# Reciprocal roots of normalisation statistics as powers on GpSimd, in a four-layer convolution block

## The chip, the cores and the metric

The kernel runs on one core of a Trainium2 chip. The metric is device time in microseconds (us) of one execution, as the median of several runs; less is better. Engines are named TensorE (PE; PEld is its loading of weights), VectorE (DVE), ScalarE (ACT), GpSimd (POOL) and SyncE (SP, which only issues DMAs here).

## The reference

The input x is 16 images of 64 channels and 128 x 128 pixels, float32. Four layers follow each other. Each normalises its input by groups (32 groups of two channels, per image) and adds its result to what came in:

```python
def _gn(v, G=32, eps=1e-5):
    g = v.reshape(B_, G, C_ // G, H_, W_)
    m = jnp.mean(g, axis=(2, 3, 4), keepdims=True)
    s = jnp.var(g, axis=(2, 3, 4), keepdims=True)
    return ((g - m) / jnp.sqrt(s + eps)).reshape(v.shape)

x = x + _L0_conv_ref(_gn(x), L0_conv_conv_w)      # gram matrix of the channels, two 64 x 64 products
x = x + _L1_conv_ref(_gn(x))                      # two 3 x 3 edge filters, sum of absolute values
x = x + _L2_conv_ref(_gn(x), L2_conv_W, L2_conv_b)  # shift by one pixel of half the channels, 3 x 3 conv
x = x + _L3_conv_ref(_gn(x), ...)                 # 3 x 3 conv, 1 x 1 conv, batch norm over all images, clip
```

The division by `jnp.sqrt(s + eps)` in `_gn` is what the change touches. The batch norm at the end has a root of its own, which it does not touch.

## The kernel before

Layers 0 and 1 are one stage, `Front`: the matrix of layer 0 and both normalisations are folded into one 128 x 128 product (`abd`) and one pair of scale and offset per channel, and the edge filters are then done by VectorE and ScalarE. `Layer2` and `Layer3` are stages with 3 x 3 convolutions on TensorE. A stage `Gram` makes the gram matrix of an image from x alone, and from it the coefficients of layers 0 and 1.

The work goes in steps, and a step in four quarters (`q` from 0 to 3). An image takes eight steps of a stage. In one step, image b is in `Front`, an earlier one in `Layer2` and a still earlier one in `Layer3`, 10 steps behind each other, with the gram matrix of a coming image beside them. The order of instructions on every engine is the one in which they are written (`InOrder` keeps it); each engine takes its own in that order and waits by semaphores for what they need.

The statistics are handled by chains, Python generators that do one link per `tick()` at the end of a quarter:

- `gram_chain` (line 313), once per image, has two roots: the first (line 347) without an epsilon, for layer 0, and the second (line 425), for layer 1, into the tile `co1`.
- `coefficients` (line 288) runs twice per image: at the end of `Front`, for layer 2, with the argument `back` (the bias), into `co2`; and at the end of `Layer2`, for layer 3, into `co`.

So there are four roots per image and 64 in all, each made by `rstd` (line 270). `mE` holds mean and mean square of each channel, in PSUM. `rstd` copies them to `me`, takes `nv` = mean squared minus mean square (the negative variance), subtracts the epsilon, has ScalarE take the root `sd`, and then, a quarter later (after the `yield`), has VectorE take the reciprocal `r0` and refine it: r = r0 * (1.5 + 0.5 * nv * r0 * r0). The offset `co[:, 1:2]` follows, and where the root itself is wanted (layers 1 and 2 keep the un-normalised input in the sum) another reciprocal makes it from r. For layer 2 it is also masked by channel (`left`, `right`).

GpSimd has this work in the steady state: in quarter 1 of each step of `Layer2`, four operations `edges` (lines 873 to 878) and two on border columns of `v` (lines 881 and 882), and, twice per step, a pair of DMAs from its queue that copy `d` into its shifted twin `qd` (`twin`, line 810). `Layer3` makes the same kind of twin with ScalarE copies (line 952). TensorE reads `d`, `qd` and `v`. VectorE makes each `d` by `difference` (line 706), and reads `edges` when it takes a result of layer 2 out of PSUM.

After the last image the statistics of the batch norm are complete, and a tail reads two arrays back from DRAM, normalises, adds and writes the output.

Of the kernel before, what the change touches and what calls it, by code (L numbers as in the profile page):

```python
# [11 lines left out]
AF = mybir.ActivationFunctionType  # L12
ALU = mybir.AluOpType
# [3 lines left out]
P = 128  # L17
# [7 lines left out]
GN_EPS = 1e-5  # L25
# [19 lines left out]
def single(table, n):  # L45

    for o in range(2):
        planes = [i for m, i, half, _ in table if (m, half) == (n, o)]
        if len(planes) == 1:
# [2 lines left out]


NAMES = [("I", P), ("same", P), ("all", P), ("gavg", P), ("gmean", P), ("bnavg", P), ("Id", C), ("q", 1),
         ("keep0", 1), ("keep1", 1), ("left", 1), ("right", 1), ("I3", 3 * P), ("lower", 1), ("upper", 1)]
AT = {}
K_END = 0
for _n, _w in NAMES:
# [19 lines left out]
def constants():  # L78
    k = np.zeros((P, K_END), np.float32)
    p = np.arange(P)  # L80
    ch = p % C

    def put(name, a):
        k[:, AT[name][0]:AT[name][1]] = a

    same = ch[:, None] == ch[None, :]
    pair = ch[:, None] // 2 == ch[None, :] // 2
    put("I", np.eye(P))
    put("same", same)
    put("all", np.full((P, P), 0.5))  # L90
    put("gavg", 0.25 * pair)
    put("gmean", pair / (2.0 * HW))
    put("bnavg", (ch[:, None] == (p // 2)[None, :]) / (B * HW))
    put("Id", ch[:, None] == np.arange(C)[None, :])
    put("q", 0.25)
    put("keep0", (~((ch >= C // 4) & (ch < C // 2)))[:, None])
    put("keep1", (~(ch < C // 4))[:, None])

    left, right = ch < C // 4, (ch >= C // 4) & (ch < C // 2)
    put("left", left[:, None])  # L100
    put("right", right[:, None])
    put("I3", np.concatenate([np.eye(P) * m[:, None] for m in (left, ~left & ~right, right)], axis=1))
    put("lower", (p < C)[:, None])
    put("upper", (p >= C)[:, None])
    return k
# [3 lines left out]
def tile_kernel(ctx: ExitStack, tc: tile.TileContext, x, cw_h, w2_t, b2, wbin_t, w1_t, b1, gamma, beta, consts, out):  # L109
    nc = tc.nc  # L110
    pe, dve, act, sp, pool = (InOrder(tc, e) for e in (nc.tensor, nc.vector, nc.scalar, nc.sync, nc.gpsimd))
# [8 lines left out]
    def k(name):  # L120
        return kc[:, AT[name][0]:AT[name][1]]
# [41 lines left out]
    def sv(name, n=1):  # L163
        return small.tile([P, n], F32, tag=name, name=name)
# [6 lines left out]
    def small_product(dst, wt, src):  # L171

        for o in (1 - last[0], last[0]):
            pe.matmul(dst[cols(o)], wt[:, cols(o)], src, start=True, stop=True)
        last[0] = o
# [5 lines left out]
    def sm(n, rows=P):  # L181
        if n > 8:
            return bank[0:rows, P:P + n]
        turn[0] = (turn[0] + 1) % 16
        return bank[0:rows, 8 * turn[0]:8 * turn[0] + n]
# [73 lines left out]
    def when(who):  # L259

        while turn_of[0] % 2 != who:
            yield
# [4 lines left out]
            if next(c, chains) is chains:  # L267
                chains.remove(c)

    def rstd(mE, r, me, eps=None):  # L270

        dve.tensor_copy(me, mE)
        nv = sv("nv")
        dve.scalar_tensor_tensor(nv, me[:, 0:1], me[:, 0:1], me[:, 1:2], op0=ALU.mult, op1=ALU.subtract)
        if eps is not None:
            dve.tensor_scalar_sub(nv, nv, eps)
        sd = sv("sd")
        act.activation(sd, nv, AF.Sqrt, scale=-1.0)
        yield
        r0 = sv("r0")  # L280
        dve.reciprocal(r0, sd)

        e = sv("e")
        dve.scalar_tensor_tensor(e, nv, r0, r0, op0=ALU.mult, op1=ALU.mult)
        dve.tensor_scalar(e, e, 0.5, 1.5, op0=ALU.mult, op1=ALU.add)
        dve.tensor_mul(r, r0, e)

    def coefficients(st, put, back=None):

        s2 = sv("s2", 2)  # L290
        dve.tensor_reduce(s2, st, axis=AX.X, op=ALU.add)
        yield
        yield from when(TENSOR)
        pm = sm(2)
        small_product(pm, k("gmean"), s2)
        yield
        co = sv("co", 2) if back is None else sv("co2", 6)
        me = sv("me", 2)
        r, mean = co[:, 0:1], me[:, 0:1]
        yield from rstd(pm, r, me, GN_EPS)  # L300
        dve.scalar_tensor_tensor(co[:, 1:2], mean, -1.0, r, op0=ALU.mult, op1=ALU.mult)
        if back is not None:

            dve.reciprocal(co[:, 2:3], r)
            dve.tensor_mul(co[:, 3:4], co[:, 2:3], k("left"))
            dve.tensor_mul(co[:, 4:5], co[:, 2:3], k("right"))
            dve.tensor_add(co[:, 5:6], mean, back)
        put(co)


# [2 lines left out]
    def gram_chain(b, pg):  # L313
# [29 lines left out]
        pm = sm(2)  # L343
        small_product(pm, k("gavg"), st)
        yield
        r, me = sv("r"), sv("me", 2)
        yield from rstd(pm, r, me)

        vv = sv("vv", 3)
# [69 lines left out]
        pm = sm(2)  # L419
# [2 lines left out]

        co = stp.tile([P, 5], F32, tag="co1", name=f"co1_{b}", bufs=EARLY + 3)
        r, mean = co[:, 0:1], co[:, 3:4]
        yield from rstd(pm, r, co[:, 3:5], GN_EPS)
        dve.scalar_tensor_tensor(co[:, 1:2], bias, mean, r, op0=ALU.subtract, op1=ALU.mult)
        dve.reciprocal(co[:, 2:3], r)
        lead[b] = abd, co

    def gram_product(pg, w, first, end):  # L430
# [16 lines left out]
    def first_gram():  # L447
# [30 lines left out]
        for link, _ in enumerate(gram_chain(0, pg)):  # L478
            if link in (2, 3, 4, 5, 6):
                rows_to_columns(1, link - 2, rows[link - 2])  # L480

    class Gram:
# [5 lines left out]
        def at(self, i, q):  # L488
            b = self.b
            n = 4 * (i - NS) + q  # L490

            self.part({1: 44, 5: 42, 9: 42}.get(n, 0))
            if n == 10:
                chains.append(gram_chain(b, self.pg))

            if i == 2 and q == 0:
                for m in range(3):
                    self.load(m)
            m = {11: 0, 13: 1, 15: 2, 19: 3, 21: 4, 23: 5, 27: 6, 31: 7}.get(4 * i + q)
            if m is not None:  # L500
                rows_to_columns(b, m, self.xr.pop(m))
                if m + 3 < NS:
                    self.load(m + 3)
# [45 lines left out]
    class Front:  # L549
# [56 lines left out]
        def at(self, i, q):  # L606
            b = self.b
            if q == 0:
                if i == -3:

                    self.xe = xin.tile([P, W], F32, tag="xe", name=f"xe_{b}", bufs=1)
                    sp.dma_start(self.xe[lo], x[b][:, HH, :])
                    sp.dma_start(self.xe[hi], x[b][:, HH - 1, :])
                    sp.dma_start(x2_d[b][0:W].rearrange("(p w) -> p w", p=1), w0[0:1, 0:W])
                if i + 3 < NS and i + 3 not in self.xs:
                    self.load(i + 3)
                if -1 <= i < NS - 1:
                    self.prepare(i + 1, 1)
                if 1 <= i:
                    self.store(i - 1)  # L620
                    act.activation(
                        junk.rearrange("p (j w) -> p j w", w=W), self.x2.pop(i - 1), AF.Square,
                        accum_out=self.st[:, 1, i - 1:i],
                    )
                if i == NS:
                    chains.append(coefficients(self.st, lambda co: coefs2.update({b: co}), b2_sb))
# [140 lines left out]
    class Layer2:  # L767
# [65 lines left out]
        def at(self, i, q):  # L833
# [3 lines left out]
            if q == 0:  # L837
                if i == NS:
                    chains.append(coefficients(self.st, self.done))
                if 1 <= i:  # L840
                    two = self.p.pop(i - 1)[0]

                    e = self.edges.pop(i - 1).rearrange("p t (m n) -> p n m t", n=2)
                    ends = two[:, :, :, 0:W:W - 1]
                    dve.tensor_add(ends, ends, e)
                    x3 = ring.tile([P, 2, CP, W], F32, tag="x3", name=f"x3_{b}_{i - 1}", bufs=NS + 2)
                    tiles3[b].append(x3)
                    dve.scalar_tensor_tensor(
                        x3.rearrange("p s j w -> p s (j w)"), two.rearrange("p s j w -> p s (j w)"), 1.0,
                        self.c.unsqueeze(1).to_broadcast([P, 2, CP * W]),  # L850
                        op0=ALU.mult, op1=ALU.add, accum_out=self.st[:, 0, i - 1:i],
                    )
                if 0 <= i < NS:
                    difference("d2", 0, self.v[i], m)
                    self.twin(0)
# [267 lines left out]
    pm = sm(2)  # L1123
    pe.matmul(pm, k("bnavg"), mv, start=True, stop=True)
    me = cpool.tile([P, 2], F32, name="me_bn")
# [4 lines left out]
    sd = cpool.tile([P, 1], F32, name="sd_bn")  # L1130
    act.activation(sd, var, AF.Sqrt)
    r0 = cpool.tile([P, 1], F32, name="r0_bn")
    dve.reciprocal(r0, sd)
    e = cpool.tile([P, 1], F32, name="e_bn")
# [56 lines left out]
```

## Time and profile before

| | us |
|---|---|
| three runs | 2726.27, 2729.09, 2729.88 |
| median | 2729.09 |
| profiled execution, span from first to last instruction | 2727.2 |
| PE busy | 2162.2 (79%) |
| DVE busy | 2170.0 (80%) |
| ACT busy | 2079.2 (76%) |
| POOL busy | 852.7 (31%) |

The profile gives the profiled execution by its span; no other time of that execution is given, and the span is 1.9 us under the median of the runs. The span divides into stages: up to 45 us the first image's gram matrix and coefficients, then the stages filling up one behind another, then all of them running together, and after about 2280 us the tail.

The shares of busy time are means over these stages, so a stage has to be looked at by itself. In a row of a timeline the figures are the start and the duration in us, then engine, line, operation and tiles (`out<-in`), and in brackets how long the engine had been idle and what ended that. Line 73 is the helper `InOrder`, through which nearly all instructions pass, so they are told apart by tile. A row of a list of waits gives the total in us, the number of waits and the longest. A group's row in an answer by tile gives minimum, median and maximum duration in ns.

### The profile page before, as it was taken

The page shows a single profiled execution, that of the slowest core. Times are in us where ns is not written, and L with a number is a line of the kernel's source. Part 1 is how long each engine was busy: PE and PEld are TensorE (multiplying, and loading weights), DVE is VectorE, ACT ScalarE, POOL GpSimd, SP SyncE. Part 2 cuts the span into 40 slices and gives each one's busy share as a digit, 9 for nine tenths or more (in the row PEclk, how much of TensorE's full clock was granted, in tenths as well). Part 3 has the DMA queues.
Part 4 walks back from the last instruction along what each step waited for, and adds up shares of the span by engine and source line. Part 5 has one row for each costly group of instructions (what it writes and reads, how often), then busy time and mean ns, then how long its engine had stood idle before and what let it go on. Part 6 is the DMA issues. An engine that isn't in the chain of part 4 may idle for free. (4 is left out here: it accounts for less than half of the span.)

```text
span 2727.2 us, 45742 instructions
## 1 busy us (share of the span) xinstructions
PE 2162.2 (79%) x14804; PEld 913.7 (34%) x14804; DVE 2170.0 (80%) x3495; ACT 2079.2 (76%) x3065; POOL 852.7 (31%) x1350
## 2 busy tenths in 40 slices
PE   6578899999999999999999999999999993000000
PEld 4234433434343434343434343333334641000000
DVE  4999999899999999999999999999995335333332
ACT  4766889898989898989898989899997667333332
POOL 2045424443434243333343334445453200000000
PEclk8689999999999999999999999999999996555555
DMA  8799878888888888888888887888877868999999
GB/s 199 205 239 239 226 197 239 225 235 225 235 228 237 227 226 229 226 227 234 225 224 237 214 204 203 207 211 216 224 200 186 226 188 314 420 420 420 420 420 385
DMA packets 693598, 685.93 MB, mean 252 GB/s; under 512 B 60096, under 2 KB 580448, under 8 KB 693360
## 3 DMA queue, kind: packets, MB, share of 16 engines
q1 hardware_dynamic: 668208, 613.83, 76.4%
q0 software_dynamic: 25152, 69.18, 10.0%
q8 instruction: 119, 1.95, 0.3%
q14 instruction: 119, 0.97, 0.1%
HBM read 346.23 MB, written 268.44 MB: 225 GB/s over the span
## 5 line engine op out<-in xcount | busy, mean ns | idle before, releaser
L73 PE MATMUL two<-d,w 128*64 128x508 f32 (+2 forms) x2560 | 848.9, 587 | 0.0
L73 PE MATMUL two<-d,wi 128*64 128x508 f32 (+3 forms) x1536 | 573.8, 577 | 0.0
L73 PE MATMUL two<-qd,pk 128*64 128x512 f32 (+1 forms) x1024 | 520.0, 589 | 24.5 <-DMA qd<-d 16.6
L73 POOL DMA_DIRECT2D qd<-d x512 | 271.1, 532 | 852.8 <-DVE d L73 323.9
L73 POOL TENSOR_SCALAR edges<-v,co 64x8 f32<-64x8 f32 x512 | 340.2, 664 | 349.0 <-ACT v L73 216.8
L73 DVE TENSOR_TENSOR d<-v 128x512 f32<-128x512 f32 (+1 forms) x512 | 346.6, 680 | 65.3 <-issue 37.5
L73 PEld LDWEIGHTS two<-d,w 128*64 128x64 f32 x2560 | 278.7, 136 | 320.0 <-issue 270.9
L73 PE MATMUL one<-v,w 128*64 128x508 f32 (+2 forms) x1600 | 364.3, 579 | 1.1 <-ACT v L73 1.1
L73 PE MATMUL one<-v,wi 128*64 128x508 f32 (+3 forms) x1536 | 353.3, 591 | 2.0 <-issue 1.4
L73 ACT COPY qd<-d 64x512 f32<-64x512 f32 x512 | 315.4, 616 | 19.9 <-DVE d L73 13.8
L73 DVE SCALAR_TENSOR_TENSOR e<-e 128x1032 f32<-128x1032 f32 (+1 forms) x256 | 313.0, 1223 | 0.0
L73 ACT ACTIVATE xh<-po,co 128x128 f32<-128x128 f32 (+1 forms) x480 | 275.9, 624 | 23.9 <-PE po L73 21.4
L73 PEld LDWEIGHTS two<-d,wi 128*64 128x64 f32 x1536 | 178.0, 135 | 197.4 <-issue 180.0
L73 DVE SCALAR_TENSOR_TENSOR y<-two,c 128x1024 f32<-128x1024 f32 x128 | 156.0, 1219 | 97.8 <-ACT v L73 45.6
L73 POOL TENSOR_SCALAR v<-v,kc 128x9 f32<-128x9 f32 x256 | 213.4, 847 | 12.0
L73 PE MATMUL po<-x,abd 64*64 64x512 f32 (+1 forms) x1024 | 177.1, 640 | 45.6 <-ACT xh L73 42.2
L73 ACT ACTIVATE v<-x,co 128x1024 f32<-128x1024 f32 (+3 forms) x256 | 203.8, 847 | 0.0
L73 ACT ACTIVATE u<-u 128x1024 f32<-128x1024 f32 x128 | 135.5, 1059 | 75.6 <-DVE u L73 74.6
L73 PEld LDWEIGHTS two<-qd,pk 128*64 128x64 f32 x1024 | 131.6, 135 | 176.9 <-issue 85.5
L73 PEld LDWEIGHTS one<-v,w 128*64 128x64 f32 x1600 | 130.9, 136 | 175.3 <-issue 146.5
L73 ACT ACTIVATE c<-one,co 128x512 f32<-128x512 f32 x128 | 86.7, 678 | 127.4 <-PE one L73 124.0
L73 DVE SCALAR_TENSOR_TENSOR u<-xh 128x1170 f32<-128x1170 f32 x128 | 175.4, 1370 | 4.2 <-ACT xh L73 4.1
(165 smaller groups left out, 3325.2 us busy)
## 6 DMA issues: line engine op xcount, KB each, us to landing
x<-in_x SPq DMA_DIRECT2D x256, 256.0 KB, 4.6
x_d<-u SPq DMA_DIRECT2D x512, 128.0 KB, 4.0
y_d<-y SPq DMA_DIRECT2D x512, 128.0 KB, 3.8
x_d<-x SPq DMA_DIRECT2D x496, 128.0 KB, 2.7
xr<-in_x SPq DMA_DIRECT2D x120, 512.0 KB, 5.9
qd<-d POOLq DMA_DIRECT2D x256, 130.0 KB, 3.3
qd<-d POOLq DMA_DIRECT2D x256, 129.8 KB, 3.8
v<-x_d SPq DMA_DIRECT2D x448, 72.1 KB, 3.0
```

Of the source, the lines that this page charges most:

```text
L73: return self.tc.keep_in_program_order(call(*args, **kwargs))
```

## The change

`rstd` no longer uses ScalarE, and VectorE's part ends with `nv`. GpSimd takes `va` = eps - `nv` and then r = `va` to the power -0.5, with the exponent from a new constant of two columns, `half`; where the root is wanted, it takes `va` to the power 0.5. For layer 2 the masked roots and the sum of mean and bias are moved from VectorE to GpSimd too. VectorE's offset `co[:, 1:2]` stays after the `yield`, and reads r.

```diff
@@ NAMES
-         ("keep0", 1), ("keep1", 1), ("left", 1), ("right", 1), ("I3", 3 * P), ("lower", 1), ("upper", 1)]
+         ("keep0", 1), ("keep1", 1), ("left", 1), ("right", 1), ("I3", 3 * P), ("lower", 1), ("upper", 1), ("half", 2)]
@@ constants
+    put("half", np.array([-0.5, 0.5]))
@@ rstd
-    def rstd(mE, r, me, eps=None):
+    def rstd(mE, r, me, eps=0.0, root=None):
 
         dve.tensor_copy(me, mE)
-        nv = sv("nv")
+        nv, va = sv("nv"), sv("va")
         dve.scalar_tensor_tensor(nv, me[:, 0:1], me[:, 0:1], me[:, 1:2], op0=ALU.mult, op1=ALU.subtract)
-        if eps is not None:
-            dve.tensor_scalar_sub(nv, nv, eps)
-        sd = sv("sd")
-        act.activation(sd, nv, AF.Sqrt, scale=-1.0)
+        pool.tensor_scalar(va, nv, -1.0, eps, op0=ALU.mult, op1=ALU.add)
+        pool.tensor_tensor(r, va, k("half")[:, 0:1], op=ALU.pow)
+        if root is not None:
+            pool.tensor_tensor(root, va, k("half")[:, 1:2], op=ALU.pow)
         yield
-        r0 = sv("r0")
-        dve.reciprocal(r0, sd)
-
-        e = sv("e")
-        dve.scalar_tensor_tensor(e, nv, r0, r0, op0=ALU.mult, op1=ALU.mult)
-        dve.tensor_scalar(e, e, 0.5, 1.5, op0=ALU.mult, op1=ALU.add)
-        dve.tensor_mul(r, r0, e)
@@ coefficients
-        yield from rstd(pm, r, me, GN_EPS)
+        yield from rstd(pm, r, me, GN_EPS, None if back is None else co[:, 2:3])
         dve.scalar_tensor_tensor(co[:, 1:2], mean, -1.0, r, op0=ALU.mult, op1=ALU.mult)
         if back is not None:
 
-            dve.reciprocal(co[:, 2:3], r)
-            dve.tensor_mul(co[:, 3:4], co[:, 2:3], k("left"))
-            dve.tensor_mul(co[:, 4:5], co[:, 2:3], k("right"))
-            dve.tensor_add(co[:, 5:6], mean, back)
+            pool.tensor_add(co[:, 5:6], mean, back)
+            pool.tensor_mul(co[:, 3:4], co[:, 2:3], k("left"))
+            pool.tensor_mul(co[:, 4:5], co[:, 2:3], k("right"))
         put(co)
@@ gram_chain
-        yield from rstd(pm, r, co[:, 3:5], GN_EPS)
+        yield from rstd(pm, r, co[:, 3:5], GN_EPS, co[:, 2:3])
         dve.scalar_tensor_tensor(co[:, 1:2], bias, mean, r, op0=ALU.subtract, op1=ALU.mult)
-        dve.reciprocal(co[:, 2:3], r)
         lead[b] = abd, co
```

## The prediction

> **What bounds the kernel now.** I read the table of windows first, since one figure for the whole span mixes stages with different limits. Columns: length, then busy us of PE, PEld, DVE, ACT, POOL, the granted clock, DMA share, GB/s.
>
> ```profile
> 30.00:45.00 15.00, 8.59 (x90) 4.96 (x88) 6.85 (x39) 7.96 (x11) 0.00 (x0) 0.66 0.95 273
> ...
> 100.00:150.00 50.00, 29.45 (x444) 19.10 (x444) 49.16 (x76) 35.05 (x50) 2.04 (x3) 0.70 0.78 197
> 150.00:300.00 150.00, 122.11 (x1174) 58.62 (x1170) 141.05 (x269) 104.65 (x146) 82.48 (x100) 0.92 0.93 238
> ...
> 1000.00:1500.00 500.00, 494.72 (x3546) 203.43 (x3543) 472.77 (x802) 450.59 (x691) 183.80 (x310) 1.00 0.86 228
> ...
> 2320.00:2727.00 407.00, 0.00 (x0) 0.00 (x0) 126.23 (x103) 127.64 (x103) 0.00 (x0) 0.50 1.01 414
> ```
>
> Four stages: to 45 us a serial chain (no engine is busy), to 300 us VectorE (49.16 of 50, 141.05 of 150), to about 2210 us TensorE (494.72 of 500), and at the end DMA alone. The changed roots stand in the first three; the tail, also written with ScalarE's root, is left as it is.
>
> Then the timeline around one root of layer 3 in TensorE's stage:
>
> ```profile
> 958.37 0.15 DVE L73 TENSOR_SCALAR nv<-nv 128x1 f32<-128x1 f32 x1
> 958.44 0.68 DVE L73 TENSOR_TENSOR d<-v 128x512 f32<-128x512 f32 x1
> ...
> 958.55 0.20 ACT L73 ACTIVATE sd<-nv 128x1 f32<-128x1 f32 x1 [0.83 <-DVE nv L73]
> ...
> 959.04 1.28 DVE L73 SCALAR_TENSOR_TENSOR u<-e,co,u 128x1024 f32<-128x1024 f32 x1
> ...
> 960.85 0.16 DVE L73 RECIPROCAL r<-sd 128x1 f32<-128x1 f32 x1
> ...
> 961.68 0.16 DVE L73 SCALAR_TENSOR_TENSOR co<-me,co 128x1 f32<-128x1 f32 x1
> ...
> 962.14 1.24 ACT L73 COPY qd<-d 64x512 f32<-64x512 f32 x2
> ...
> 963.44 0.64 PE L73 MATMUL two<-qd,pk 128*64 128x512 f32 x1 [0.70 <-ACT qd L73]
> ```
>
> See three things. ScalarE stood 0.83 us until nv came. VectorE came back for the root 2.33 us later (958.52 to 960.85) without a wait, and spent 0.83 us on four dependent small operations. TensorE lost 0.70 us because ScalarE's copy qd was late. The last is one of TensorE's few waits, by the list of waits of 430 to 1760 us:
>
> ```profile
> PE two L73 <- ACT qd L73: 7.0, 13, 0.7
> PE two L73 <- DMA qd<-d: 6.6, 10, 1.3
> ```
>
> The price of a small GpSimd operation is that of edges (minimum, median, maximum):
>
> ```profile
> L73 POOL TENSOR_SCALAR edges<-v,co x512: 302/320/3487, 152.2 to 2176.2; 64x8 f32<-64x8 f32 x171
> ```
>
> **What the Trainium skill says.** "SBUF — State Buffer", section "Who interferes with whom": a VectorE instruction with two SBUF inputs and a GpSimd instruction that reads SBUF exclude each other, and the second to issue blocks. The trace agrees: the median of edges is 0.32 us but the groups give a mean of 0.664, and the first four, beside VectorE's u and e of 1.2 us each, took 7.47 us together. "GPSIMD Engine Reference", section 2.1: the first call into freshly loaded code pays about 6 us. In the built program one library instruction stands ahead of GpSimd's first TENSOR_SCALAR in both kernels. Before, that was at 152.21 us, 0.1 us after its input, so the load hid in 43.9 us of idleness; now it follows the memset at 21.67 us, with 12 us until the first nv at 33.79. I count nothing. "ScalarE: Activation LUTs", "What ACT_TABLE_LOAD costs": 1283 ns per load; the trace has one of 1283 ns, and it stays, since the start and the tail still take a Sqrt. No page prices a power on GpSimd, and the trace has none.
>
> **The unknown.** Call p the time of one undisturbed 128x1 power. Below, 0.30 us (the fastest edges; no power is quicker than a multiply). Above, 4.8 us: the GPSIMD page's section 2 gives a core 16 partitions, and if its code took them one after another at a whole small operation each, 16 x 0.30. I take 0.8: one vector of 16 lanes, and two to three simple operations' worth of steps.
>
> **The change by parts.** VectorE loses 384 instructions: 64 each of reciprocal (156 ns), e (220), e (154) and product (159), which by starts is 0.83 us per root; 48 subtractions of 154; 32 reciprocals into co; 32 products and 16 additions of some 155. By kind, per root: 0.8 us (first root of a Gram chain, no epsilon), 1.15 (its second), 1.5 (layer 2), 1.0 (layer 3); 16 of each. ScalarE loses 64 roots of 0.20 us and the waits for nv, 36.5 us in 30 places. GpSimd gains 208 instructions, no DMA: 64 va, 64 powers, 32 root powers, 48 for left, right and the bias. SP's queue is passed by nothing.
>
> The new wait: VectorE's product into co waits for the first power alone (the second is awaited by no near VectorE instruction). The latency is hand-over, va, hand-over, power, hand-over: 0.07 + 0.32 + 0.07 + p + 0.07 = 0.53 + p undisturbed, 0.07 being the step from edges to edges. Beside VectorE's long operations, va and the power each end at an operation's end. Behind va on GpSimd stand edges, the border columns of v and the twin DMAs; VectorE's d waits for those columns.
>
> *First chain (to 45 us), serial.* First root: VectorE goes on at once with vv, which doesn't need r; 33.79 to 34.77 us drops out, -1.0; r is wanted at 36.88 and is there at 35.1. Second: nv at 41.79 to co at 43.08 was 1.29 us, becomes 0.53 + 0.8 = 1.33. Sum **-0.9**.
>
> *45 to 300 us, VectorE.* Eleven roots (4, 4, 2, 1 of the kinds): 4 x 0.8 + 4 x 1.15 + 2 x 1.5 + 1.0 = 11.8 us of VectorE less. New stalls, by the time from nv to the use in the trace: the four first roots have none (r is used a product later); of the others, those with 5.67 and 7.12 us have none; 4.62 and 2.85 us about 0.5 each; 2.51 and 1.72 us 0.2 + p = 1.0 each (va takes the time of VectorE's own operations, then the power is bare); 1.12 us (148.43) 0.5 + p = 1.3. Together 4.3, net -7.5. VectorE is 94% the bound there: **-6.8** (bounds -9 at p = 0.3, +11 at 4.8).
>
> *300 to 2210 us, TensorE.* VectorE's and ScalarE's saved time is covered by TensorE's work. What counts is TensorE's 7.0 us of waits for qd, nearly all behind a root of layer 3, where ScalarE now runs 0.9 us earlier: -6.5. Against that, a root of layer 3 stalls VectorE for 0.2 + p = 1.0, just what it saves. After a chain's second root, the power and the root power stand before edges, which start up to 1 us later; the columns were ready 3.7 us before VectorE's d, so that is hidden. At other steps d waits already (15 times, 4.0 us), but no root is there. For twin DMAs, which TensorE waits for at times (6.6 us), I add 1.5. Sum **-5.0**. End (layer 3 at 2205.8 us): 1.53 becomes 1.5; ScalarE earlier by 0.3: **-0.3**.
>
> Total -0.9 - 6.8 - 5.0 - 0.3 = **-13.0** against the profiled span: 2727.2 - 13.0 = 2714.2. The runs' median is 1.9 above that span, which I keep: **2716**.
>
> **Rivals.** (a) *Likeliest, 0.48*: as summed, p up to 1.2; its own range 2710 to 2724. For it: VectorE and ScalarE bound the start, GpSimd is 31% busy. (b) *Slower, 0.37*: the power is long. Past 0.8 us every us of p costs about 1 (first chain) + 4.5 (start) + 12 (one root of layer 3 in each of twelve batches, past what VectorE saves, with the next twin on TensorE's path, as the waits for qd show) + 1.5 (end) = 19. So the sum is nothing at p = 1.5 and slower than 0.2% at 1.8. At p = 2.4 it is -13 + 30 = +17, and with two powers ahead of edges d waits about 1 us more per batch: +29, or 2758. At 4.8 about 2805. For it: the contended edges, and a twin's DMA that TensorE waits for; against it, VectorE's 5% slack. (c) *No change, 0.15*: p between 1.2 and 1.8, the start's gain eaten by the stalls later, 2724 to 2734.
>
> **How the numbers follow.** About 0.2%, 5.5 us, is what a measurement can tell from no change. The cases give 0.48 faster, 0.15 same, 0.37 slower. The range begins at p = 0.3 with all waits for qd gone (-0.5 - 2.2 - 2.3 more: -18, or 2711; 2709 with the runs' spread) and reaches into (b) to 2755, past which I leave some 15 in 100.
>
> **What would show it.** The power's row gives p. Right: no ACT sd row, TensorE's waits for qd near nothing, VectorE's waits for GpSimd small, the 300 us mark some 8 us earlier and the period of a batch 132.0 us or a little less. Wrong: a power over 1.5 us, VectorE's co waiting for GpSimd in every batch, a longer period, TensorE waiting for twins; or a first power some 6 us late, at 34 us.

## The result, and the profile after

| | before | changed |
|---|---|---|
| median of the runs beside each other | 2729.49 (4 runs, 2726.27 to 2730.86) | 2714.52 (4 runs, 2713.5 to 2721.25) |
| profiled execution: own time, span | span 2727.2 | 2713.5, span 2711.7 |
| DVE busy, instructions | 2170.0, 3495 | 2116.7, 3111 |
| ACT busy | 2079.2 | 2069.4 |
| POOL busy | 852.7 | 1042.6 |

The ratio of the times is 0.9954, with a 95% interval of 0.994 to 0.9968. Predicted were 2716 us and a gain of 13.0 us; by spans it was 15.5. The marks and experiments below show that this agreement is the sum of two errors of opposite sign.

The table of windows of the changed kernel, its columns as before: length, busy us of PE, PEld, DVE, ACT, POOL, granted clock, DMA share, GB/s.

```profile
30.00:45.00 15.00, 9.73 (x104) 5.32 (x100) 5.30 (x30) 8.69 (x11) 2.03 (x5) 0.77 1.16 281
...
100.00:150.00 50.00, 30.39 (x464) 19.16 (x460) 48.59 (x69) 35.79 (x50) 13.88 (x16) 0.72 0.79 203
150.00:300.00 150.00, 120.86 (x1118) 57.24 (x1118) 133.17 (x221) 103.75 (x140) 97.34 (x123) 0.91 0.93 239
...
1000.00:1500.00 500.00, 493.19 (x3556) 202.19 (x3556) 462.67 (x708) 451.31 (x681) 236.14 (x363) 1.00 0.90 231
```

VectorE is busy 7.9 us less from 150 to 300 us (133.17 against 141.05). But TensorE has started no more matmuls by 300 us than before (2344 against 2343), so that stage gave almost nothing.

The groups of GpSimd's new operations, with minimum, median and maximum in ns:

```profile
L73 POOL TENSOR_TENSOR co<-va,kc x80: 541/1144/1495, 41.0 to 2189.5; 128x1 f32<-128x1 f32 x80
L73 POOL TENSOR_SCALAR va<-nv x64: 182/564/4735, 34.1 to 2188.9; 128x1 f32<-128x1 f32 x64
L73 POOL TENSOR_TENSOR r<-va,kc x16: 548/1437/1441, 34.4 to 1659.2; 128x1 f32<-128x1 f32 x16
```

So p, the undisturbed power, is 0.54 us; beside VectorE's long operations it becomes 1.1 to 1.5. Now the timeline around the same root of layer 3:

```profile
952.28 0.25 DVE L73 SCALAR_TENSOR_TENSOR nv<-me 128x1 f32<-128x1 f32 x1
952.46 0.70 DVE L73 TENSOR_TENSOR d<-v 128x512 f32<-128x512 f32 x1
952.76 0.46 POOL L73 TENSOR_SCALAR va<-nv 128x1 f32<-128x1 f32 x1
...
953.30 1.49 POOL L73 TENSOR_TENSOR co<-va,kc 128x1 f32<-128x1 f32 x1
...
954.29 0.68 DVE L73 TENSOR_TENSOR d<-v 128x512 f32<-128x512 f32 x1
954.89 0.15 DVE L73 SCALAR_TENSOR_TENSOR co<-me,co 128x1 f32<-128x1 f32 x1
...
959.14 0.69 DVE L73 TENSOR_TENSOR d<-v 128x512 f32<-128x512 f32 x1
...
960.38 1.03 POOL L73 DMA_DIRECT2D qd<-d  x2 [3.85 <-PE po L73]
```

VectorE comes back to co at 954.89 and has no idle time in brackets: the power ended at 954.79, just in time. The last two rows belong to what the prediction priced at 1.5 us. VectorE's d at 959.14 is Layer2's (n = 0), and its twin is a DMA pair. By the list of waits from 430 to 1760 us, TensorE has lost its waits for ScalarE, and waits longer for those twins (7.0 and 6.6 us before):

```profile
PE two L73 <- DMA qd<-d: 16.2, 10, 2.5
```

By starts of like instructions the changed kernel leads by 1.1 us at 41 us, by 0.4 at 301, by 4.5 at 562, by 9.0 at 1486, by 17.1 at 2205, and by 15.5 at the end.

### The profile page after: what moved, and what is told of

Its sections match the earlier page's. It is cut to its first block, busy times and chain, and to the rows that moved or that the text cites. A ratio compares the mean times of both kernels' runs of the same rounds, so it can differ in the third digit from the quotient of the medians.

```text
span 2711.7 us, 45518 instructions
## 1 busy us (share of the span) xinstructions
PE 2146.4 (79%) x14804; PEld 905.4 (33%) x14804; DVE 2116.7 (78%) x3111; ACT 2069.4 (76%) x3001; POOL 1042.6 (38%) x1558
## 5 line engine op out<-in xcount | busy, mean ns | idle before, releaser
L73 PE MATMUL two<-d,w 128*64 128x508 f32 (+2 forms) x2560 | 835.7, 586 | 0.0
L73 POOL TENSOR_SCALAR edges<-v,co 64x8 f32<-64x8 f32 x512 | 328.7, 642 | 274.7 <-ACT v L73 195.1
L73 PEld LDWEIGHTS two<-d,w 128*64 128x64 f32 x2560 | 272.4, 136 | 322.8 <-issue 282.7
L73 ACT COPY qd<-d 64x512 f32<-64x512 f32 x512 | 315.6, 616 | 23.3 <-DVE d L73 13.8
L73 POOL TENSOR_SCALAR v<-v,kc 128x9 f32<-128x9 f32 x256 | 229.9, 912 | 12.0
```

The lines of the kernel that those rows point to most:

```text
L73: return self.tc.keep_in_program_order(call(*args, **kwargs))
```

## The experiments

I had three theories after this. **A**: the gain in TensorE's stage is ScalarE's freedom at layer 3's root. **B**: it is VectorE's shorter work. **C**: the start's gain was eaten because va and the powers stand ahead of the edges and border columns on GpSimd. All runs are in this table; a kernel's ratio is against the kernel before on the same chip.

| kernel | median (runs) | lowest to highest | ratio, 95% interval |
|---|---|---|---|
| e1: layer 3's 16 roots alone | 2729.81 (13) | 2726.7 to 2733.8 | 1.0002 (0.9994 to 1.001) |
| e2: the other 48 alone | 2724.09 (21) | 2720.3 to 2729.5 | 0.9981 (0.9974 to 0.9987) |
| e3: layers 2 and 3, Gram roots as before | 2725.05 (21) | 2716.3 to 2730.5 | 0.9979 (0.9972 to 0.9985) |
| e4: changed, VectorE's work put back | 2731.70 (13) | 2725.6 to 2738.7 | 1.0007 (0.9998 to 1.0015) |
| e5: changed, ScalarE's root put back | 2716.37 (5) | 2714.8 to 2716.7 | 0.9953 (0.994 to 0.9966) |
| e6: changed, first power twice | 2728.27 (13) | 2723.6 to 2734.1 | 1.0 (0.9992 to 1.0008) |
| e7: changed, Gram roots behind edges | 2724.29 (20) | 2718.7 to 2729.8 | 0.9982 (0.9976 to 0.9989) |
| e8: changed, offsets to GpSimd too | 2722.68 (7) | 2716.0 to 2727.2 | 0.9973 (0.9962 to 0.9983) |
| e9: changed, again | 2718.16 (5) | 2711.2 to 2721.0 | 0.9956 (0.9944 to 0.9969) |
| e10: changed, d first | 2706.65 (5) | 2705.8 to 2708.0 | 0.9917 (0.9904 to 0.9931) |
| e11: before, d first | 2728.61 (13) | 2726.1 to 2729.7 | 0.9998 (0.9989 to 1.0006) |
| e12: layer 3's roots alone, d first | 2718.13 (5) | 2716.2 to 2719.2 | 0.9961 (0.9946 to 0.9975) |

### The change in two parts: e1, e2, e3

In each, `rstd` has both ways, chosen by the caller:

```diff
-    def rstd(mE, r, me, eps=0.0, root=None):
+    def rstd(mE, r, me, eps=0.0, root=None, on_pool=True):
...
+        if on_pool:
             pool.tensor_scalar(va, nv, -1.0, eps, op0=ALU.mult, op1=ALU.add)
             pool.tensor_tensor(r, va, k("half")[:, 0:1], op=ALU.pow)
...
+        act.activation(sd, nv, AF.Sqrt, scale=-1.0)
```

e1 has `on_pool` for layer 3 alone. What was expected of it:

> Only the 16 roots of layer 3 are powers on GpSimd; the 48 others stay with ScalarE's root and VectorE's refinement. Theory A (the gain of TensorE's stage comes from ScalarE no longer standing at layer 3's root): the wait of TensorE for ScalarE's qd behind that root goes, the period of an image in TensorE's stage is about 131.2 us, and the total is 8 to 11 us under the kernel before. Theory B (the gain comes from VectorE's shorter work at all 64 roots): a quarter of it, 3 to 5 us under, period 131.6. Both: the 300 us mark as before or up to 1 us earlier.

e2 has it for the Gram chains and layer 2:

> The 48 roots of the gram chains and of layer 2 are powers on GpSimd; layer 3's 16 stay as before. Theory A: TensorE's wait of about 0.7 us for ScalarE's qd stays in every image, period about 131.8 to 132, total 2 to 5 us under the kernel before. Theory B: three quarters of the gain, 10 to 12 us under, period about 131.2.

e3 has it for layers 2 and 3:

> The 32 roots of the gram chains stay as before, those of layers 2 and 3 are powers on GpSimd. Theory C (between 150 and 300 us va and the power stand on GpSimd ahead of edges and of v's border columns, and VectorE's d waits for the columns): those waits of 0.9 to 1.3 us, one for each gram root, are gone, so the 300 us mark is no later than with the whole change although these roots cost VectorE 0.7 to 0.8 us each again; the first chain is 1.2 us slower. Total within 3 us of the changed kernel on either side. Rival: the columns are late for another cause, the waits stay, and the total is 4 to 8 us slower than the changed kernel, since 32 roots' worth of VectorE's time comes back.

In e1 ScalarE's part did all that A asks, and the time did not move. Its list of waits, 430 to 1760 us:

```profile
PE two L73 <- DMA qd<-d: 19.5, 9, 2.7
```

Of the 7.0 us of waits for ScalarE none is left, but the waits for twins rose from 6.6 to 19.5. A alone falls. e2 came out 6.1 us under the kernel before, between what A (2 to 5) and B (10 to 12) gave it. e3's waits of VectorE from 45 to 300 us show that C's mechanism is there, since they fall back once the Gram roots don't stand ahead of the edges; first the changed kernel, then e3 (before: 2.2, 3 times):

```profile
DVE d L73 <- POOL v L73: 7.4, 8, 1.3
...
DVE co L73 <- POOL co L73: 2.6, 4, 0.7
```

```profile
DVE d L73 <- POOL v L73: 2.5, 3, 1.4
```

Yet the nv that stood at 301.3 us before (the mark at 300 us from here on) is at 302.5 in e3, no earlier: VectorE's waits for ScalarE's u are 5.5 us there instead of 0.5. (Two executions of the changed kernel have this mark at 300.9 and 298.4, so a difference of 2 us between single profiles says little.) Its time, 7 to 11 us above the changed kernel, is not what C gave it (within 3 us). One thing stands out: 0 for layer 3's roots and -6 for the other 48 don't make -12 or -15. The gains of the parts do not add up to that of the whole.

### Which engine's work counts: e4, e5

e4 puts the refinement's four VectorE operations back, on values that nobody reads; e5 puts ScalarE's root back, into a tile that nobody reads. Both come after the powers in `rstd`.

```diff
         yield
+        z0, z = sv("z0"), sv("z")
+        dve.reciprocal(z0, nv)
+        dve.scalar_tensor_tensor(z, nv, z0, z0, op0=ALU.mult, op1=ALU.mult)
+        dve.tensor_scalar(z, z, 0.5, 1.5, op0=ALU.mult, op1=ALU.add)
+        dve.tensor_mul(z, z0, z)
```

> The changed kernel, with VectorE again doing the four small operations of the refinement at every root, on values that nobody uses (0.83 us at each of 64 roots); ScalarE stays free of the roots. Theory A: TensorE's stage keeps its gain, and the total is 2 to 5 us slower than the changed kernel (the first chain and the start lose theirs). Theory B: the gain is lost, the total is within 3 us of the kernel before.

```diff
+        act.activation(sv("sd"), nv, AF.Sqrt, scale=-1.0)
         yield
```

> The changed kernel with ScalarE's root of 0.20 us put back at each of the 64 places, into a tile that nobody reads, waiting for nv as before; VectorE and GpSimd are left as in the change. Theory B (what counts in TensorE's stage is VectorE's shorter work): ScalarE's wait and root come back, TensorE waits for ScalarE's qd by some 6 us again in 430 to 1760 us and less for the twin DMAs (below 12 us), and the time stays within 3 us of the changed kernel's, 2713 to 2718. Theory A' (ScalarE's freedom is worth something once VectorE is short, so both are needed): half of the gain or more goes, 2721 or more. VectorE's work put back in the same way cost all of it.

VectorE's 0.7 us per root cost the whole gain, while ScalarE's root cost nothing that can be measured. Both are B's answers. In e5 ScalarE's lateness is back, and what TensorE waits for it, it waits less for the twins (16.2 us in the changed kernel):

```profile
PE two L73 <- DMA qd<-d: 9.0, 8, 2.1
PE two L73 <- ACT qd L73: 6.3, 9, 0.8
```

So the two waits stand in a row, and the later one takes up what the earlier one gives.

### The price of the power, and its place: e6, e7, e8

e6 takes the first power twice:

```diff
+        pool.tensor_tensor(sv("r9"), va, k("half")[:, 0:1], op=ALU.pow)
         pool.tensor_tensor(r, va, k("half")[:, 0:1], op=ALU.pow)
```

> The changed kernel with the first power of each root taken twice on GpSimd, one after the other, the first into a tile that nobody reads: r comes p later, and everything behind it on GpSimd too. The slope of the prediction, 19 us per us of p past 0.8, puts p = 1.08 (twice 0.54) at +5 to +6 us, about 2720. If VectorE's wait for r is still covered at nearly every root, as the near absence of waits at co in the changed kernel suggests, and only the edges and border columns come later, in the start: +1 to +3 us, 2715 to 2718, with the 300 us mark 1 to 2 us later and the period of an image unchanged. If the powers take 1.1 to 1.5 us each beside VectorE's long operations, and that counts: +10 or more.

Of the three answers, the third came: 10 to 14 us more than the changed kernel, for a second power of 0.54 us (by the records GpSimd's time grew by 0.70 us per root). And there was something that I had not looked for. TensorE in e6, in the timeline:

```profile
972.29 1.03 PE L73 MATMUL two<-d,wi 128*64 128x508 f32 x4
975.46 1.09 PE L73 MATMUL two<-qd,pk 128*64 128x512 f32 x1 [2.15 <-DMA qd<-d]
975.47 1.11 PE L73 MATMUL two<-d,wi 128*64 128x508 f32 x1
976.34 1.06 PE L73 MATMUL two<-qd,pk 128*64 128x512 f32 x1
976.37 1.05 PE L73 MATMUL two<-d,wi 128*64 128x508 f32 x1
977.20 1.05 PE L73 MATMUL two<-d,w 128*64 128x508 f32 x1
```

and in windows around that place (the granted clock is the third figure from the end):

```profile
973.50:975.40 1.90, 0.00 (x0) 0.00 (x0) 1.90 (x4) 1.90 (x3) 1.66 (x5) 1.00 1.07 325
975.40:979.00 3.60, 3.54 (x10) 1.21 (x12) 3.60 (x6) 3.59 (x8) 1.62 (x1) 0.53 0.76 211
979.00:982.50 3.50, 3.50 (x20) 1.22 (x18) 3.47 (x6) 3.43 (x6) 1.28 (x3) 1.00 0.85 247
```

After a wait of 2.15 us four pairs of matmuls start 0.86 us apart, at a clock of 0.53, and then the step is 0.43 again: some 1.7 us more, on top of the wait. The same wait in the changed kernel was 1.40 us (966.31), with full clock behind it. The Trainium skill, "TensorE: Matmul & The Clock Gate", section "What's actually happening", says that the clock goes to half after an idle window of about 3.4 us that runs free of the kernel. That it comes and goes between runs is seen here too; that it needs 3.4 us is not: in the profiled executions, from 430 us on, it came after waits of 2.0 to 3.5 us, but not after all of them (2.25 and 2.47 us in the changed kernel and 2.68 in e1 were at full clock), and after none below 2.0. Slow pairs from 312 to 2205 us, and their cost over 0.43 us each (a count can be off by one or two, by where a burst is taken to end):

| before | changed | e1 | e2 | e3 | e4 | e5 | e6 | e7 | e8 | e9 | e10 to e12 |
|---|---|---|---|---|---|---|---|---|---|---|---|
| 0 | 0 | 19, 7.0 us | 0 | 11, 4.1 | 13, 4.8 | 0 | 19, 7.4 | 18, 6.7 | 3, 1.1 | 10, 3.6 | 0 |

The changed kernel's waits lie around this edge. e7 and e8 were meant to improve it. e7 lets the edges go first:

```diff
+        if behind and turn_of[0] % 4 == 1:
+            yield
         pool.tensor_scalar(va, nv, -1.0, eps, op0=ALU.mult, op1=ALU.add)
```

> The changed kernel with GpSimd's va and powers of a Gram chain's roots issued one quarter later where they stood ahead of quarter 1 (from the chain of image 2 on), so that the edges and border columns of v of that quarter go first on GpSimd. Theory C (the start's gain was eaten by VectorE's d waiting for border columns behind va and the powers): d's waits for v in 45 to 300 us go from 7.4 us back to 3 or less, the 300 us mark comes 4 us or more earlier (297 or before), and the time falls by 3 to 5 us, to 2710 or less. Rival: the start is bound by something else by then (the arrival of x or the twins), the waits move to another place, and the time is within 1.5 us of the changed kernel's.

The wait for border columns fell as C says, and came back at co, which now waits for a power that is behind the edges (45 to 300 us of e7):

```profile
DVE co L73 <- POOL co L73: 8.3, 6, 2.6
...
DVE d L73 <- POOL v L73: 2.9, 5, 1.4
```

The mark at 300 us is 302.1. The sum of the two waits, 11.2 us, is no less than the changed kernel's 10.0: whichever of the two goes second on GpSimd, VectorE waits for it. The time, 2724.3 in the median of 20 runs, is 6 to 10 us above the changed kernel's, which neither C nor the rival expected. Its profile has 6.7 us of slow pairs, but that execution was the slowest of the 20; what made the others late stays open.

e8 moves five more VectorE operations per image to GpSimd:

```diff
-        dve.scalar_tensor_tensor(co[:, 1:2], mean, -1.0, r, op0=ALU.mult, op1=ALU.mult)
+        pool.tensor_scalar(co[:, 1:2], mean, r, -1.0, op0=ALU.mult, op1=ALU.mult)
...
-                dve.tensor_scalar_mul(edge[half], co, k(half))
+                pool.tensor_scalar_mul(edge[half], co, k(half))
```

> The changed kernel with 48 offsets co[:, 1:2] and 32 masked copies of co (edge) moved from VectorE to GpSimd as well: five more small VectorE operations of 0.16 us less per image, 0.8 us, against 4.45 us that the change took off, and VectorE then waits for no power. Theory B: 0.8 / 4.45 of what the change gained in TensorE's stage, 2 to 3 us less, 2712, the period of an image 130.8 or less. Rival: GpSimd's longer chain (some 1 us more per root, ahead of edges and twin DMAs) gives that back or more: 2714 or above, with d's waits for v and TensorE's waits for twin DMAs longer.

The rival holds by the median. The profiled execution (2716.5) was among its fastest, with TensorE's waits for twins at 13.8 us, less than the changed kernel's, so the longer waits that the rival named are not seen, and what its slower executions have stays open.

### The twin out of the way: e9 to e12

What starts TensorE again in the longest wait of an image is the twin of Layer2's d (n = 0). For each kernel I took from the starts and landings in its trace, counted from nv of layer 3's root in eight images (562 to 1486 us), when the twin's first DMA is issued, when its pair has landed, and when TensorE is done with what it has before it:

| kernel | issued, mean | landed, mean | TensorE ready, median | landed less ready |
|---|---|---|---|---|
| before | 9.1 | 13.9 | 13.6 | 0.3 |
| changed; e9 | 8.1; 8.1 | 14.2; 14.1 | 12.6; 12.6 | 1.6; 1.5 |
| e1 | 8.1 | 14.6 | 12.6 | 2.0 |
| e2 | 9.1 | 14.6 | 13.6 | 1.0 |
| e3 | 8.1 | 14.4 | 12.6 | 1.8 |
| e4 | 8.8 | 14.5 | 12.6 | 1.9 |
| e5 | 8.1 | 14.3 | 13.4 | 0.9 |
| e6 | 8.6 | 14.6 | 12.6 | 1.9 |
| e7 | 8.2 | 14.4 | 12.6 | 1.8 |
| e8 | 7.7 | 14.0 | 12.6 | 1.3 |
| e10 | 6.5 | 13.1 | 12.6 | 0.5 |
| e11 | 7.5 | 13.6 | 13.6 | 0.0 |
| e12 | 6.5 | 13.3 | 12.6 | 0.7 |

Where ScalarE's lateness is gone, TensorE is ready at 12.6 instead of 13.6. The twin was issued a microsecond earlier too (8.1 for 9.1), but didn't land earlier. A window of the changed kernel from issue to landing, and one of the kernel before, have this (the DMA engines' share is the last figure but one):

```profile
960.40:966.20 5.80, 4.50 (x22) 1.27 (x18) 5.80 (x8) 5.61 (x7) 4.70 (x7) 1.00 1.05 292
```

```profile
967.20:971.90 4.70, 4.48 (x22) 1.27 (x18) 4.70 (x5) 4.54 (x5) 3.76 (x5) 1.00 1.10 320
```

The DMA engines are full there: by the timeline SyncE has just issued the four stores of Front's result and issues those of layer 3's y. That a twin issued sooner waits among them fits this; no run took the stores away, so it is argued. The landing doesn't follow the issue alone: e2's twins, issued like those of the kernel before, land 0.7 us later.

e9 is the changed kernel again. In e10 to e12, d and its twin go ahead of the sum x3, in the changed kernel, in the kernel before, and in e1:

```diff
                 if i == NS:
                     chains.append(coefficients(self.st, self.done))
+                if 0 <= i < NS:
+                    difference("d2", 0, self.v[i], m)
+                    self.twin(0)
                 if 1 <= i:
...
-                if 0 <= i < NS:
-                    difference("d2", 0, self.v[i], m)
-                    self.twin(0)
```

> The changed kernel once more, unaltered, beside more runs of the kernel before on the same chip, to narrow the ratio 0.9954 [0.994, 0.9968] and to see how far one execution's waits for twin DMAs differ from another's. If the first result was typical: 2713 to 2717, TensorE's waits for the twin after layer 3's root between 1.3 and 2.5 us each, and no half-speed matmuls behind them. If it was lucky (waits of over 2 us were followed by three or four pairs of matmuls at 0.86 us instead of 0.43 in kernels that came out 6 to 14 us slower): up to 2721, with such pairs in some images.

> The changed kernel with one thing moved in quarter 0 of Layer2: VectorE's d (n = 0) and its twin DMAs are issued ahead of the addition of edges and the sum x3 of the step before, so d comes about 2 us earlier. Theory B' (in TensorE's stage an image's time is TensorE's work plus its wait for the twin of the d that follows layer 3's root, d + 0.6 + 5 to 6 us of DMA against TensorE's arrival 12.6 us after nv): those waits, 16.2 us in ten places of 430 to 1760 us, fall below 5 us, the period of an image goes from 130.95 to 129.5 or so, and the time to about 2700 (2694 to 2706). Rival: the place isn't the limit; d then waits for TensorE's reading of the old d, or x3 comes later and TensorE waits for its PSUM buffers instead; 2713 or above.

> The kernel before with the order of quarter 0 of Layer2 alone altered (d and its twin ahead of the sum x3), none of the change. In the kernel before TensorE arrives at that twin about 13.6 us after nv of layer 3's root, a microsecond later than in the changed kernel, since it has waited for ScalarE's qd; its waits for twins are 6.6 us and for ScalarE's qd 7.0 us in 430 to 1760 us. Theory B' (two waits of an image in a row, and the later one takes up what the earlier one gives): only the twins' part goes, 5 to 7 us, 2722 to 2724, and the waits for ScalarE's qd stay at 7 us. Rival (the order alone is what made 2706, and the power does nothing there): 2710 or less.

> Powers on GpSimd for layer 3's 16 roots alone (by itself 2729.8, no gain), with d and its twin ahead of the sum x3. Theory B': with the twin out of the way the time that ScalarE gains at layer 3's root, some 7 us of TensorE's waits, is no longer given back, so it comes out 6 us or more below the kernel before with the same order, at about 2716, with neither wait above 2 us in total. Rival (ScalarE's earlier qd is worth nothing anyhow): within 2 us of the kernel before with the same order.

e9 gave the first ratio again (0.9956), with ten slow pairs in its profile: the first profile, with none, was on the good side. e10 comes out at 2706.65 us, just above what B' gave it (2694 to 2706), with a period of 130.4 us (129.5 was expected). In it the twin is issued 1.6 us earlier and lands 1.1 earlier; TensorE's waits from 430 to 1760 us, against 16.2:

```profile
PE two L73 <- DMA qd<-d: 5.2, 7, 1.8
PE two L73 <- ACT qd L73: 0.2, 1, 0.2
```

That is a version that beats both kernels, 22.6 us under the kernel before and 11.5 under the changed kernel on the same chip. e11 shows that the order alone is worth nothing. I had expected 5 to 7 us: the twin's waits fell by 4.1 us, but TensorE was held by ScalarE as before:

```profile
PE two L73 <- ACT qd L73: 7.6, 13, 0.7
PE two L73 <- DMA qd<-d: 2.5, 6, 0.8
```

e12 has little left of the waits for ScalarE, 8.1 us of those for twins (under 2 was expected, e1 had 19.5), and no slow pair:

```profile
PE two L73 <- DMA qd<-d: 8.1, 8, 1.7
PE two L73 <- ACT qd L73: 1.0, 2, 0.6
```

Layer 3's roots alone: -0.4 us. The order alone: 0.1. Both: -10.4, or 0.65 per root. So A falls as it was put and returns as half of a pair: what layer 3's roots give is real, but only where the twin doesn't follow late. (The sums of these waits in e11 and e12, 10.1 and 9.1 us, are nearly alike; the period of an image, 131.7 and 130.7 us, is not. Waits that such a list doesn't have are shown below.) What of e12's gain is ScalarE's and what VectorE's share at these roots, e12 doesn't tell.

## Why the prediction was right, and where it was not

The total was right by luck: the start gave 5.5 to 7.8 us less than was counted, and TensorE's stage 5.0 to 11.6 more.

**p.** Taken 0.8 us, measured 0.54. No library load delayed the first va: it started at 34.14 us, took 0.19, and the power followed at once. The price of a small operation beside VectorE's long ones was foreseen (va: median 0.56, power 1.1 to 1.5).

**First chain, -0.9.** -1.1 by the second root's nv (41.57 to 40.44), -1.5 by its co (43.08 to 41.61). The step holds, with p shorter than taken: from the end of nv to co it was 0.95 us, where 1.33 was counted.

**45 to 300 us, -6.8: wrong.** Measured +1.0 in the first profile and -1.3 in e9 (leads of 0.43 and 2.94 us at 301 us, less the 1.47 and 1.65 of the first chain). The working has two slips of its own: a root of layer 2 comes to 1.6 us by its parts and not 1.5, and 94% of 7.5 is 7.05. VectorE's work did fall: it had 63 instructions less from 45 to 300 us, as counted, and was busy 7.5 us less (231.3 against 238.9); but its idle time grew by 10.8 us (13.3 to 24.1). The stalls at co were even shorter than counted (2.6 against 4.3). The step that failed is the one that kept edges and border columns out of the sum: "the columns were ready 3.7 us before VectorE's d" is a fact of TensorE's stage, and I had not asked it of the start. There the two powers of a Gram chain's second root stand ahead (the timeline of the changed kernel):

```profile
225.60 2.54 POOL L73 TENSOR_TENSOR co<-va,kc 128x1 f32<-128x1 f32 x2
228.15 3.15 POOL L73 TENSOR_SCALAR edges<-v,co 64x8 f32<-64x8 f32 x4
231.40 0.62 POOL L73 TENSOR_SCALAR v<-v,kc 128x9 f32<-128x9 f32 x2
232.05 0.69 DVE L73 TENSOR_TENSOR d<-v 128x512 f32<-128x512 f32 x1 [1.30 <-POOL v L73]
```

In all, d's waits for v rose by 5.2 us (2.2 to 7.4), about half of what VectorE's idle time grew by. e3 and e7 showed this wait go and another take its place, so the whole loss is not put down to it.

**300 to 2210 us, -5.0: the sign right, the size and the reason wrong.** Measured -16.6 in the first profile and -10.0 in e9 (leads of 0.4 to 17.1, and of 2.9 to 12.9). Three steps failed.

- "VectorE's and ScalarE's saved time is covered by TensorE's work." For ScalarE e5 agrees, given the late twin. For VectorE e4 refutes it: the same 0.7 us per root put back cost 13.5 to 17 us. By its marks against the first profile 1.4 us of that lie before 301 us, 7.1 from there to 562, and 6.4 in the next eight images; slow pairs, 4.8 us, are part of it. VectorE's slack is real over an image, but not at every place in it: in e4 the twin is issued 0.7 us later (8.8 for 8.1). As it lands only 0.2 us later, how VectorE's work reaches TensorE is not shown in full.
- "-6.5" for the waits for qd: they vanished as said, but in e1 this alone was worth nothing: TensorE then waits for a twin that lands no earlier, and 7.0 us of slow pairs follow those waits. The 7.0 us were also not all that ScalarE's lateness costs, as the next lines show.
- "+1.5" for twin DMAs: measured +9.6. The twin was named and then priced by a guess; its landing, and the full DMA engines, could have been read in the trace of before.

That the stage gained although TensorE's waits of over 0.25 us sum to about the same (16.7 us in 24 before, 16.2 in 10 after, 312 to 2205 us) has to do with waits that the list doesn't have. TensorE's matmuls run in pairs, one of each half of the columns. When the operand of one half is late, the other half goes on alone, and TensorE isn't idle. Before:

```profile
975.85 1.24 ACT L73 COPY qd<-d 64x512 f32<-64x512 f32 x2
976.28 1.02 PE L73 MATMUL two<-d,w 128*64 128x512 f32 x2
977.14 0.64 PE L73 MATMUL two<-qd,pk 128*64 128x512 f32 x1
977.14 0.64 PE L73 MATMUL two<-d,w 128*64 128x508 f32 x1
```

ScalarE's copy ends at 977.09, and the first matmul that reads it starts at 977.14; two matmuls of the other half have gone ahead, 0.43 us apart. In the changed kernel the copy (from 969.05, 1.25 us) ends at 970.30, before TensorE is there, and the same place is paired from the start:

```profile
970.60 0.59 PE L73 MATMUL two<-d,w 128*64 128x512 f32 x1
970.63 0.59 PE L73 MATMUL two<-qd,pk 128*64 128x512 f32 x1
```

Before, this image has four such starts at the end of a ScalarE copy (959.95, 963.44, 977.14, 979.60), and only the one at 963.44 is in the list. From there to the next po, the two groups of matmuls took 5.57 us (959.73 to 965.30) and 5.28 (976.28 to 981.56) against 4.37 and 4.40 in the changed kernel, 2.08 us more; the group that waits for the twin took 4.77 against 5.87, 1.10 us less. Net 0.98 us, of the 1.03 by which this image is shorter in the changed kernel. Over eight images it is the same. Windows from 562 us, before and changed (the second figure is the length, the third PE's busy time):

```profile
562.32:1616.58 1054.26, 1043.77 (x7358) 424.46 (x7356) 1000.54 (x1673) 953.36 (x1461) 392.83 (x657) 1.00 0.86 227
557.79:1605.37 1047.58, 1032.98 (x7352) 418.70 (x7350) 973.48 (x1481) 948.43 (x1430) 496.57 (x761) 1.00 0.89 229
```

For the same matmuls TensorE is busy 1.35 us less per image (130.47 to 129.12) and idle 0.52 more (1.31 to 1.83): the period goes from 131.78 to 130.95. Of the starts at the end of a ScalarE copy there are 29 in these images before and none after. The same split tells e11 (130.61 busy, 1.08 idle) from e12 (129.81, 0.86). So the 6.5 us priced what a list of idle time shows and not the whole of ScalarE's lateness. Yet in e5 that lateness is back at layer 3's root without cost, so what it is worth hangs on the twin behind it.

Outside layer 3's roots, four waits of TensorE in the kernel before are gone (1.35 us at 412, 0.60 at 1694, 1.37 at 1719, 1.26 at 1757), another 4.6 us.

**End, -0.3.** 1.6 us (2.1 in e9) were given back between 2205 us and the end, where DMA bounds: a miss of 1.9 (2.4).

**Rivals.** The long power (b) did not come, as p is under 1.2. Its mechanism is in e6's trace: VectorE waits 12.2 us at co for the power from 300 to 2205 us (27 times), where the changed kernel waits once, 0.7 us. e6's 10 to 14 us for 0.54 us are 19 to 25 us per us of p, against 19 predicted; but 7.4 us of them are slow pairs in its profile, which the prediction didn't have, so that the slopes agree is in part luck. The flat part below 0.8 is not there.

## What to carry to other kernels

When a wait on the bounding engine goes, look for the next wait in that engine's own order and price it with the same care: of two waits in a row, either alone may be worth nothing, and both together 10 us, as here. A list of idle time doesn't show a wait of half an engine; compare the time that the same work takes. An engine with slack on average can be late at one place; moving the producer ahead of work that nobody is waiting for there costs no instruction. For what comes by DMA, read the landing, not the issue. An engine that takes over small operations has a queue too, and what stood first in it comes later.

## What was not expected of the hardware

- TensorE's clock went to half (0.53 granted over 3.6 us) for about 3.5 us after pauses from 2.0 us on, not each time. Kernels with slow pairs in their profile spread widely from run to run (e4 over 13 us in 13 runs, e6 over 10), e10 and e5 little (2.3 and 1.9, in 5 runs each); but e2, with no slow pair in its one profile, spread over 9 in 21. That the clock makes the spread is not shown.
- When one of TensorE's column halves (64 columns each here) waits and the other works, TensorE counts as busy: for the same matmuls it was busy 1.35 us longer per image in the kernel before.
- A 128x1 power on GpSimd takes 0.54 us, under two of edges' multiplies (0.32), and a library load ahead of it was nowhere to be seen.
- In the changed kernel a DMA of a twin (130 KB) landed 3.5 us after issue in the median of 430 to 1620 us, but 5.1 to 6.4 at the place where TensorE waited for it, in each of eight images (3.7 to 5.3 there in the kernel before): with the DMA engines full, an issue 1.0 us earlier was no earlier landing, and one 1.6 us earlier gained 0.3 (e11) or 1.1 (e10).
